# Scratch image by row, channel, column: fewer and longer runs into the patches of a depthwise convolution

## The chip, the cores and the metric

The kernel runs on one core of one Trainium2 chip. All data are float32. The metric is the time of one execution on the device in microseconds. The profile is of one execution, and its times count from its first instruction.

## The reference, cut to what matters

A batch of 16 images of 256 channels and 64 x 64 pixels goes through two layers. Layer 0 is a group norm, an RMS norm over channels, linear attention with four heads, an output projection, an RMS norm, and a residual. Layer 1 is a group norm and a mixture of four experts, of which a router picks two for each image; each expert is a depthwise 3 x 3 convolution, an exact GELU and a pointwise product over channels.

```python
def _expert(x, dw_k, dw_b, pw_k, pw_b):
    h = lax.conv_general_dilated(x, dw_k, window_strides=(1, 1), padding='SAME', feature_group_count=x.shape[1], ...)
    h = h + dw_b[None, :, None, None]
    h = jax.nn.gelu(h, approximate=False)
    h = jnp.einsum('bchw,oc->bohw', h, pw_k) + pw_b[None, :, None, None]
    return h
...
x = x + _L0_conv_ref(_gn(x), ...)
x = x + _L1_conv_ref(_gn(x), ...)
```

## The kernel before, in words

The work of an image is cut into phases, and up to several images are under way at once. Phase "in" takes the statistics of the first group norm, with loads `load_a` (tile xa, L945). Phase "q" normalises (`load_b`, tile xb, L948), projects and builds the attention's context. Phase "out" applies it and adds to the image, which stays in `ring` (loaded in L824). Phase "route" computes the router. Phases "c", "v" and "x" are layer 1, and its output is stored in L1483.

The 256 channels of the depthwise convolution are split. VectorE computes channels 128 to 255 with eight multiply-adds for each tile of 16 rows (`tap1`, L1436). TensorE computes channels 0 to 127 in phase "c", half an image (32 rows) at a time, h = 0 and 1:

- `pad0` writes the normalised rows of a half into `pd0`, with a border: 128 channels in the partitions, and in each 18 rows (`WR`) of 132 elements (`SW`). These 132 are two padded strips of 66, for the upper and the lower 16 rows of the half.
- `lay` (L1350) stores `pd0` in a scratch image in HBM, `lays[h]`.
- `spread` (L1359) reads the scratch image back into a patch buffer `xr`, so that the 3 x 3 window lies in the partitions: partition 18 dx + u holds row u shifted by dx columns, 54 partitions in all, for a group of channels; r = 0 and 1 put two groups of channels at partitions 0 and 64. Partition 54 keeps ones, for the bias.
- `conv0` (L1394) multiplies a channel's patch with the channel's banded tap matrix `taps`. One product gives 16 output rows for both chosen experts.
- `gelu0` (L1406), `put` (L1411) and `take` (L1422) apply GELU, store the result in a second scratch, `hids[h]`, and read it back with channels in the partitions as tile hp, which the pointwise products (L1465) use.

Before, `CB` is 16: a patch holds 16 channels at r = 0 and 16 at r = 1, so a half has `NU` = 4 patches. There are `NXR` = 2 patch buffers. A patch is read with six transfers, for each r and each dx, with 18 rows of 16 runs each; a run is 130 elements, 520 bytes.

All these transfers are issued by SyncE (SP) in one queue. The order of all instructions on all queues is written out: `rows` lists every step with a phase, an image and a key, `place` gives it a due time from the table `PLAN` (base values by key, and exceptions for single images), and the steps are issued in the order of these times. A unit of `PLAN` is a 64th of an image's period. The schedule is manual, so an engine never runs a step ahead of one that stands before it in its queue.

Of the kernel before, what the change touches and what calls it, by code (L numbers as in the profile page):

```python
# [10 lines left out]
FP = mybir.dt.float32  # L11
# [5 lines left out]
P = 128  # L17
# [11 lines left out]
QR = H // NQ  # L29
# [13 lines left out]
WR = QR + 2  # L43
WK = 3 * WR
KT = WK + 1
# [3 lines left out]
CB = 16  # L49
NU = P // (2 * CB)  # L50
NXR = 2
# [9 lines left out]
    "load_x1": 2.47, "mean": 6.06, "means": 12.14, "dev": 15.13, "devs": 17.94, "scale": 19.64,  # L61
    "bias": 22.84, "in_lead": 26.32, "norm0": -8.37, "norm1": -3.84, "turn_x0": 0.8, "x_sq0": 1.94,
    "x_sq1": 2.47, "turn_x1": 1.77, "x_sq2": 2.71, "x_sq3": 3.45, "token": 4.3, "x_keep0": 5.16,
    "x_keep1": 5.18, "x_keep2": 5.25, "x_keep3": 5.28, "project0": 3.33, "evacuate0": 5.95,
    "project1": 4.22, "evacuate1": 6.41, "project2": 4.36, "evacuate2": 6.69, "project3": 4.83,
    "evacuate3": 6.79, "context": 9.85, "q_sum": 8.95, "q_norm": 10.71, "q_turn": 14.88,
    "q_keep": 16.51, "mix_a": 10.1, "mix_turn": 10.19, "mix_v": 10.58, "mix_vv": 11.37,
    "mix_b": 11.59, "mix_out": 13.76, "mix_c": 14.28, "mix_lead": 16.01, "attend0": -1.55,
    "out_sq0": -0.08, "out_sq1": 0.23, "out_scale0": 0.69, "out_norm0": 2.07, "attend1": -0.02,
    "out_sq2": 1.36, "out_sq3": 1.4, "out_scale1": 2.39, "out_norm1": 3.75, "out_turn0": 5.8,  # L70
    "out_add0": 7.08, "sq_sums0": 8.58, "out_turn1": 6.3, "out_add1": 7.4, "sq_sums1": 9.3,
    "sums1": 10.09, "means1": 10.12, "scale1": 11.26, "router": 11.97, "route": 12.07,
    "choose": 13.45, "pick_taps": 21.11, "route_lead": 21.97, "weigh": 23.15, "pick_bias": 26.54,
    "pad1": -9.33, "start0": -0.79, "tap01": 1.45, "tap02": 1.68, "tap03": 2.04, "tap04": 2.27,
    "tap05": 2.38, "tap06": 5.02, "tap07": 5.53, "tap08": 6.45, "gelu10": 13.51, "start1": 2.19,
    "tap11": 3.82, "tap12": 8.44, "tap13": 8.46, "tap14": 9.11, "tap15": 9.48, "tap16": 12.72,
    "tap17": 13.76, "tap18": 14.53, "gelu11": 15.1, "pw00": 16.39, "pw01": 16.8, "pw02": 17.78,
    "pw03": 17.67, "pw10": 16.24, "pw11": 16.38, "pw12": 20.17, "pw13": 20.98, "residual00": 20.37,
    "residual01": 20.58, "store0": 32.42, "residual10": 22.66, "residual11": 22.95, "store1": 24.52,
    "in_first": 0.94, "in_more": 1.71, "q_first": 3.44, "out_first": 48.37, "out_more": 9.94,  # L80
    "q_less": 0.19, "load_a0": -17.65, "load_a1": -7.44, "load_b0": -16.6, "load_b1": -6.03,
    "stats0": -12.91, "stats1": -1.7, "load_weights": 29.84, "scale_weights": 28.54,
    "end_pw00": 102.59, "end_pw01": -70.76, "end_pw02": 22.48, "end_pw03": 218.26,
    "end_residual00": 0.34, "end_residual01": 51.45, "end_pw10": 154.95, "end_pw11": -20.19,
    "end_pw12": -67.04, "end_pw13": -35.14, "end_residual10": -34.02, "end_residual11": 60.24,
    "x_0": 0.93, "x_1": 0.16, "x_2": -0.1, "x_e1": 3.92, "x_e2": 4.69, "route_0": -3.24,
    "route_1": -0.18, "route_2": 0.26, "route_e1": -0.52, "route_e2": -0.36, "out_0": -5.57,
    "out_1": -0.5, "out_2": -0.02, "out_e1": -2.04, "out_e2": -0.91, "q_0": -6.4, "q_1": -1.79,
    "q_2": 0.02, "q_e1": -1.76, "q_e2": -0.97, "in_0": -31.7, "in_1": 8.38, "in_2": 3.12,
    "in_e1": -1.71, "in_e2": 0.13, "pw04": -118.21, "pw14": -3.07, "x_last": 16.29, "v_last": 15.03,  # L90
    "v_e1": 2.91, "tap18@e2.3": 12.85, "start0@e1.3": -3.52, "token@2.7": 3.88, "x_sq2@2.2": 3.74,
    "gelu11@e1.2": 14.77, "tap03@0.1": 1.16, "tap01@2.0": 1.08, "project0@0.0": 0.61,
    "out_norm1@2.7": 4.05, "out_sq1@e2.0": 0.67, "out_scale1@1.2": 2.97, "evacuate0@1.2": 5.59,
    "context@1.7": 8.56, "out_scale1@0.0": 4.31, "q_norm@0.0": 12.2, "out_turn0@1.4": 6.57,
    "mix_turn@0.7": 10.41, "token@2.1": 5.01, "out_sq3@1.6": 2.23, "project0@2.7": 4.76,
    "context@0.5": 10.29, "context@0.7": 8.85, "attend1@e1.3": -1.81, "out_norm1@1.1": 2.82,
    "context@2.1": 9.04, "q_norm@0.6": 10.76, "out_turn0@e1.5": 6.51, "out_norm0@1.1": 2.17,
    "gelu11@e2.3": 14.74, "evacuate2@1.7": 6.56, "out_norm1@0.6": 3.44, "evacuate2@2.2": 7.77,
    "project0@2.3": 2.36, "token@2.2": 3.83, "norm0@0.0": -11.77, "token@0.0": 2.08,
    "q_sum@0.0": 11.89, "x_sq2@2.6": 1.49, "norm1@0.0": -4.6, "out_norm1@e1.1": 3.47,  # L100
    "x_sq2@1.2": 3.52, "tap04@e2.2": 2.34, "x_keep0@0.5": 5.79, "out_turn0@1.2": 4.48,
    "evacuate3@1.7": 7.41, "q_sum@e2.4": 9.13, "x_sq2@2.5": 4.05, "turn_x0@0.0": -3.21,
    "out_scale0@1.2": 2.66, "tap13@2.0": 7.09, "x_keep3@1.2": 4.83, "mix_vv@2.7": 12.07,
    "out_turn0@1.3": 3.88, "q_sum@e2.6": 9.1, "x_sq2@0.0": 1.95, "scale1@0.0": 10.63,
    "token@0.1": 2.9, "q_sum@1.5": 10.12, "q_sum@1.1": 8.65, "tap12@e1.1": 4.38,
    "x_keep1@0.1": 7.82, "evacuate2@1.6": 5.85, "q_sum@1.3": 8.96, "out_turn0@2.6": 5.62,
    "out_turn0@1.1": 2.84, "route@0.0": 11.68, "x_sq2@1.4": 2.92, "q_turn@0.2": 14.91,
    "bias@0.7": 22.58, "token@1.4": 4.28, "pick_taps@e1.0": 15.29, "out_add0@2.5": 5.94,
    "means@0.7": -2.13, "dev@e2.7": 2.44, "evacuate3@1.2": 8.83, "x_sq3@1.4": 3.69,
    "x_keep1@0.7": 6.7, "mix_turn@1.7": 10.31, "x_sq2@2.7": 3.86, "x_sq3@2.5": 3.02,  # L110
    "mix_v@0.7": 10.76, "token@1.1": 4.28, "tap17@e2.3": 12.01, "out_turn0@e1.1": 6.18,
    "token@0.2": 5.57, "token@2.6": 5.19, "q_sum@1.2": 9.27, "out_norm0@1.2": 3.9,
    "x_keep0@0.7": 5.29, "mix_b@e1.7": 12.97, "choose@1.0": 15.45, "project0@e1.7": 3.62,
    "out_norm1@1.2": 4.35, "tap07@e1.2": 9.83, "tap11@e1.2": 5.06, "means@1.7": 3.63,
    "token@1.3": 3.21, "out_scale0@1.0": 2.27, "q_sum@e1.6": 9.24, "tap12@e2.0": 7.96,
    "out_scale1@e1.1": 1.65, "out_scale0@1.3": 0.78, "route@e1.0": 12.38, "x_sq2@1.5": 2.61,
    "pick_taps@2.0": 15.11, "out_turn0@1.0": 5.78, "scale@0.7": 19.8, "tap06@e1.0": 4.95,
    "out_turn1@e2.2": 7.26, "token@0.7": 4.82, "q_sum@e2.7": 9.92, "stats0@e2.5": -8.11,
    "tap13@e1.1": 5.09, "out_turn0@1.5": 6.39, "token@e1.5": 3.87, "token@1.6": 4.36,
    "q_turn@e2.1": 14.75, "out_norm1@e2.5": 2.7, "turn_x0@2.4": -0.38, "out_scale0@1.4": -1.04,  # L120
    "out_add1@0.5": 5.86, "out_add1@1.0": 8.63, "weigh@0.0": 25.58, "x_sq2@1.0": 2.93,
    "token@1.5": 3.15, "pick_bias@2.0": 25.19, "out_turn0@0.3": 6.25, "turn_x0@2.2": -2.86,
    "mix_b@0.7": 11.76, "out_scale1@e2.6": 2.43, "gelu11@e1.0": 17.17, "token@e2.7": 3.47,
    "out_sq3@0.6": 1.42, "context@1.2": 15.45, "q_sum@e2.0": 8.11, "tap01@e1.3": 0.02,
    "choose@e1.0": 13.66, "tap12@e2.2": 8.32, "x_keep0@0.1": 4.83, "x_sq2@1.6": 2.27,
    "load_a1@1.6": -8.35, "q_sum@0.1": 13.46, "q_sum@2.5": 10.2, "q_norm@0.2": 14.38,
    "tap13@e2.3": 7.78, "weigh@2.0": 20.53, "x_sq2@1.1": 2.49, "q_sum@e2.3": 9.79,
    "x_keep0@1.2": 9.93, "stats1@1.0": 2.95, "tap03@1.1": 1.88, "q_sum@1.0": 8.1,
    "q_turn@0.6": 13.24, "project1@2.2": 5.21, "token@1.2": 3.7, "context@1.4": 11.85,
    "mean@1.7": 0.59, "tap03@e1.2": -0.05, "x_sq3@2.7": 3.41, "x_keep2@0.4": 7.31, "token@2.4": 3.5,  # L130
    "q_turn@e2.3": 15.38, "mix_b@1.7": 12.57, "tap15@e1.2": 9.1, "out_sq3@e2.5": 1.53,
    "load_a1@1.4": -8.23, "x_sq3@1.6": 3.7, "pick_bias@1.0": 32.6, "q_sum@1.7": 8.15,
    "tap03@e1.3": 1.72, "out_norm1@0.7": 4.24, "choose@2.0": 13.4, "q_norm@0.3": 12.98,
    "out_turn0@0.1": 6.17, "x_keep1@0.5": 6.37, "out_turn0@e1.7": 7.03, "out_norm1@0.5": 3.66,
    "router@2.0": 11.71, "means1@e1.0": 10.8, "mean@0.7": -5.23, "project0@e2.7": 3.52,
    "x_keep0@1.7": 6.08, "context@1.3": 10.11, "router@0.0": 11.34, "tap17@e1.3": 15.47,
# [2110 lines left out]
```

## Time and profile before

| | |
|---|---|
| median of the runs | 2900.73 us (2875.53, 2900.73, 2912.88) |
| profiled execution: time, span | 2905.06 us, 2903.3 us |
| granted TensorE clock, mean | 0.929 |
| PE, DVE, ACT, POOL busy | 85%, 78%, 71%, 31% of the span |
| transfers of SP's queue (q1) | 498336 packets, 573.80 MB, 75.2% of 16 engines |
| HBM read, written | 400.94 MB, 175.24 MB |
| PE idle until a patch lands (xr<-lay) | 182.6 us in 64 waits |
| issue of one spread transfer on SP | 265 ns shortest, 742 median, 3787 longest |

The span reaches from the first to the last instruction. "A <- B" after a wait names who ended it; "DMA xr<-lay" is a transfer from lay to xr, and "SPq" is the time in which SP's queue issues or waits. A DMA share is the mean over 16 DMA engines, so it can hide that some of them are fuller than others. The chain that ended last is followed back from the last instruction; its shares say what the end of the program waited for.

### The profile page before, as it was taken

How to read it: one execution, taken by the hardware profiler on the slowest of the kernel's cores; microseconds unless marked ns; L12 is line 12 of the kernel's file. 1: busy time of each engine (PE TensorE's matmuls, PEld its weight loads, DVE VectorE, ACT ScalarE, POOL GpSimd, SP SyncE). 2: the span in 40 equal slices, each digit the busy share in tenths (PEclk: the TensorE clock that was granted, in tenths of full speed). 3: DMA queues.
4: the chain of work that ended last, by engine and by line, in shares of the span. 5: the costliest groups of instructions: out<-in, count | busy, mean ns of one | idle time of the engine just before them, and what ended most of it. 6: DMA issues, size and time to landing. Idle time of an engine off the chain costs nothing.

```text
span 2903.3 us, 49820 instructions
## 1 busy us (share of the span) xinstructions
PE 2478.1 (85%) x17204; PEld 1660.5 (57%) x17204; DVE 2255.1 (78%) x3489; ACT 2067.3 (71%) x4852; POOL 886.9 (31%) x1206
## 2 busy tenths in 40 slices
PE   6888888899788898888898888899889888896876
PEld 5775555566465666556566565566656556553432
DVE  7556787887778887888887778798887877677785
ACT  3697777787777887777687777788778778775432
POOL 4343243332223232232333223333223333232110
PEclk9998999999999999999999899999999999998888
DMA  4857887787877887887778887778788767777775
GB/s 136 128 160 185 210 209 192 206 222 206 215 190 211 218 222 211 221 212 198 212 206 227 208 209 203 204 222 222 214 228 215 196 186 190 180 180 193 196 190 153
DMA packets 531925, 579.57 MB, mean 200 GB/s; under 512 B 63184, under 2 KB 424144, under 8 KB 523472
## 3 DMA queue, kind: packets, MB, share of 16 engines
q1 hardware_dynamic: 498336, 573.80, 75.2%
q10 hardware_dynamic: 33328, 2.49, 1.5%
q8 instruction: 139, 2.28, 0.3%
q14 instruction: 122, 1.00, 0.1%
HBM read 400.94 MB, written 175.24 MB: 198 GB/s over the span
## 4 chain that ended last, share of the span: by engine, by line
DMA 32%; PE 30%; DVE 12%; ACT 9%; SPq 9%; issue 4%; POOL 3%; ACTq 0%; DVEq 0%; POOLq 0%
DMA xr<-lay 15%; PE pw L1465 10%; DMA hid<-hx 8%; SPq L1359 7%; DVE acc L1436 5%; DMA hp<-hid 5%; PE pq L1036 5%; PE dw L1394 4%; PE po L1130 4%; PE pc L1054 3%; PE px L1005 2%; DMA lay<-pd 1%; ACT junk L1138 1%; DMA xa<-in_x 1%; ACT hx L1406 1%
## 5 line engine op out<-in xcount | busy, mean ns | idle before, releaser
L1436 DVE SCALAR_TENSOR_TENSOR acc<-pd,ds,acc 128x1024 f32<-128x1024 f32 x1024 | 1325.8, 1299 | 79.3 <-ACT acc L1429 63.7
L1465 PE MATMUL pw<-acc,ps 128*128 128x512 f32 x1024 | 512.0, 635 | 31.2 <-ACT acc L1444 28.1
L929 POOL TENSOR_SCALAR s<-ss 128x2 f32<-128x2 f32 x256 | 117.6, 459 | 1366.3 <-ACT junk L1138 1363.2
L1465 PE MATMUL pw<-hp,ps 128*128 128x512 f32 x1024 | 495.4, 617 | 32.4 <-DMA hp<-hid 31.3
L1036 PE MATMUL pq<-wqkv_n,xg 128*128 128x256 f32 x2048 | 494.5, 386 | 13.1 <-DVE ring L1167 5.3
L1036 PEld LDWEIGHTS pq<-wqkv_n,xg 128*128 128x128 f32 x2048 | 383.0, 192 | 91.2 <-issue 20.0
L1138 ACT ACTIVATE junk<-po 128x256 f32<-128x256 f32 x512 | 198.2, 387 | 302.6 <-PE po L1130 283.6
L1394 PE MATMUL dw<-xr,taps 55*32 55x128 f32 x8192 | 209.8, 317 | 213.6 <-DMA xr<-lay 182.6
L1465 PEld LDWEIGHTS pw<-acc,ps 128*128 128x128 f32 x1024 | 195.1, 201 | 229.8 <-issue 154.1
L1465 PEld LDWEIGHTS pw<-hp,ps 128*128 128x128 f32 x1024 | 193.7, 198 | 229.7 <-issue 218.6
L1394 PEld LDWEIGHTS dw<-xr,taps 55*32 55x32 f32 x8192 | 153.4, 121 | 296.2 <-issue 194.9
L1130 PE MATMUL po<-mw,qt 128*128 128x256 f32 x1024 | 289.3, 410 | 12.1 <-ACT ob L1151 2.3
L1480 DVE SCALAR_TENSOR_TENSOR ring<-pw,bs,ring 128x512 f32<-128x512 f32 x248 | 181.8, 745 | 130.2 <-PE pw L1465 123.3
L1153 DVE TENSOR_TENSOR ob<-po,s 128x512 f32<-128x512 f32 x208 | 141.6, 682 | 159.5 <-POOL s L930 156.0
L1406 ACT ACTIVATE hx<-dw 128x512 f32<-128x512 f32 x256 | 149.8, 597 | 159.3 <-PE dw L1394 100.6
L1012 ACT ACTIVATE jx<-px 128x256 f32<-128x256 f32 x512 | 197.7, 386 | 85.4 <-PE px L1005 75.9
L1167 DVE SCALAR_TENSOR_TENSOR ring<-tr,gout,ring 128x512 f32<-128x512 f32 x256 | 186.3, 744 | 89.9 <-PE tr L1158 82.5
L1054 PE MATMUL pc<-xt,e 128*128 128x257 f32 x1024 | 253.1, 390 | 1.9 <-ACT xt L1023 1.4
L930 POOL TENSOR_TENSOR s<-s,mhalf 128x2 f32<-128x2 f32 x256 | 243.8, 952 | 21.3
L1130 PEld LDWEIGHTS po<-mw,qt 128*128 128x128 f32 x1024 | 195.5, 204 | 80.5 <-issue 38.4
L1044 ACT ACTIVATE e<-pq,r 128x256 f32<-128x256 f32 x512 | 210.5, 477 | 30.5 <-PE pq L1036 20.3
L1054 PEld LDWEIGHTS pc<-xt,e 128*128 128x128 f32 x1024 | 193.4, 196 | 34.4 <-issue 6.7
(145 smaller groups left out, 3562.3 us busy)
## 6 DMA issues: line engine op xcount, KB each, us to landing
xr<-lay SPq DMA_DIRECT2D x768, 146.2 KB
hid<-hx SPq DMA_DIRECT2D x256, 256.0 KB
hp<-hid SPq DMA_DIRECT2D x128, 512.0 KB
out<-ring SPq DMA_DIRECT2D x128, 512.0 KB
xa<-in_x SPq DMA_DIRECT2D x240, 256.0 KB
xb<-in_x SPq DMA_DIRECT2D x240, 256.0 KB
ring<-in_x SPq DMA_DIRECT2D x120, 512.0 KB
lay<-pd SPq DMA_DIRECT2D x32, 1188.0 KB
```

The lines of the kernel that those rows point to most:

```text
L930: nc.gpsimd.tensor_tensor(out_t, out_t, mhalf[:, :n], ALU.pow)
L1012: nc.scalar.activation(junk[:, :C], live["px", b, g, c // 2][:, c % 2], AF.Square, accum_out=ss[:, c : c + 1])
L1036: nc.tensor.matmul(pq, xg[:, k, c * P : (c + 1) * P], wqkv[:, k, : 2 * HID], start=(k == 0), stop=(k == KH - 1),)
L1044: nc.scalar.activation(live["e", b, g][:, c], live["pq", b, g, c // 2][:, c % 2], AF.Exp, scale=live["r", b, g][:, c : c + 1],)
L1054: nc.tensor.matmul(live["pc", b], live["e", b, g][:, c, HID:], xt[g % 2][:, c], start=(g == 0 and c == 0), stop=(g == NG - 1 and c == CG - 1),
L1130: nc.tensor.matmul(po[:, c], qt[:, n * P : (n + 1) * P], live["mw", b], start=True, stop=True)
L1138: nc.scalar.activation(junk[:, :C], live["po", b, g, hf][:, c], AF.Square, accum_out=ss[:, c : c + 1])
L1167: nc.vector.scalar_tensor_tensor(xin, live.pop(("tr", b, g, k)), gout[:, k : k + 1], xin, ALU.mult, ALU.add, accum_out=live["sm", b][:, 0, ...
L1359: nc.sync.dma_start(out=xr[(h * NU + v) % NXR][k0 : k0 + WR], in_=src[c0 : c0 + CB, :, dx : dx + SW - 2].rearrange("c u x -> u c x"),)
L1394: nc.tensor.matmul(pair[r][g * 2 * QR : (g + 1) * 2 * QR, s * HC : (s + 1) * HC], taps[ks, CB * v + i].rearrange("p i x -> p (i x)"), stri ...
L1436: nc.vector.scalar_tensor_tensor(acc, pd1[j % 2][:, t // 3 : t // 3 + QR, t % 3 : t % 3 + W], live["ds", b][:, i, t : t + 1], acc, ALU.mul ...
L1465: nc.tensor.matmul(po, w, rhs, start=begin, stop=end)
```

## The change

The scratch image is laid out by row, channel and column in place of channel, row and column. `lay` writes each channel's 18 rows to 18 places. In the new layout, eight channels of one row lie one after the other, 8 x 132 elements, so a row of a patch, shifted by dx, is one run of 1054 elements, 4216 bytes. A patch holds eight channels at each r, a half has eight patches, and there are four buffers. `spread` reads a patch with two transfers, one for each r, whose source steps over dx, then u, then the run, and whose destination is 54 partitions. `conv0` computes half of a pair of PSUM banks for each patch, and `put` still stores 16 channels at a time. The table `PLAN` has new values for nearly every key, and keys for the added patches; the lines shown are those of phase "c".

```diff
-CB = 16
+CB = 8
 NU = P // (2 * CB)
-NXR = 2
+NXR = 4
...
-    "lay": -4.49, "take00": 14.65, "take01": 13.96, "take10": 15.38, "take11": 16.26,
-    "c_lead": 0.53, "pad00": -8.92, "pad01": -7.63, "spread0": 2.48, "spread1": -1.79,
-    "spread2": 6.12, "spread3": 7.74, "conv0": 2.5, "gelu000": 4.29, "put00": 6.25, "gelu001": 4.71,
-    "put01": 6.61, "conv1": 5.01, "gelu010": 7.37, "put10": 8.3, "gelu011": 8.18, "put11": 9.1,
-    "conv2": 8.29, "gelu020": 10.86, "put20": 13.38, "gelu021": 10.21, "put21": 11.72,
-    "conv3": 12.34, "gelu030": 12.97, "put30": 14.03, "gelu031": 13.31, "put31": 14.24, "c_0": 0.71,
...
+    "pick11": 11.29, "lay": -3.67, "take00": 14.67, "take01": 12.36, "take10": 15.56,
+    "take11": 15.71, "c_lead": 0.55, "pad00": -9.35, "pad01": -7.2, "spread0": 1.78,
+    "spread1": -1.99, "spread2": -0.01, "spread3": 3.78, "spread4": 5.62, "spread5": 6.59,
+    "spread6": 7.67, "spread7": 7.97, "conv0": 2.42, "conv1": 2.77, "gelu000": 4.44, "put00": 5.71,
+    "gelu001": 5.41, "put01": 7.94, "conv2": 4.71, "conv3": 4.75, "gelu010": 6.6, "put10": 8.6,
+    "gelu011": 6.97, "put11": 10.06, "conv4": 8.45, "conv5": 8.51, "gelu020": 10.87, "put20": 12.36,
+    "gelu021": 10.39, "put21": 12.22, "conv6": 11.92, "conv7": 11.92, "gelu030": 12.14,
...
-    xr = [const.tile([P, CB, SW - 2], FP, name=f"xr_{i}") for i in range(NXR)]
+    xr = [const.tile([P, CB, SW], FP, name=f"xr_{i}") for i in range(NXR)]
...
-    lays = [hbm.tile([P, WR * SW], FP, tag=f"lay{h}", name=f"lay_{h}", bufs=1) for h in range(2)]
+    lays = [hbm.tile([WR, P, SW], FP, tag=f"lay{h}", name=f"lay_{h}", bufs=1) for h in range(2)]
...
     def lay(b, h):
-        nc.sync.dma_start(out=lays[h], in_=pd0.rearrange("p u a w -> p (u a w)"))
-
-    def spread(b, h, v):
-
-        src = lays[h].rearrange("p (u x) -> p u x", u=WR)
+        nc.sync.dma_start(
+            out=lays[h].rearrange("u p x -> p u x"), in_=pd0.rearrange("p u a w -> p u (a w)")
+        )
+
+    def spread(b, h, t):
+
+        n = CB * SW - 2
+        tile_t = xr[(h * NU + t) % NXR].rearrange("p c x -> p (c x)")
         for r in range(2):
-            c0 = r * P // 2 + CB * v
-            for dx in range(3):
-                k0 = r * P // 2 + dx * WR
-                nc.sync.dma_start(
-                    out=xr[(h * NU + v) % NXR][k0 : k0 + WR],
-                    in_=src[c0 : c0 + CB, :, dx : dx + SW - 2].rearrange("c u x -> u c x"),
-                )
+            c0 = r * P // 2 + CB * t
+            run = lays[h][:, c0 : c0 + CB].rearrange("u c x -> u (c x)")[:, :n]
+            nc.sync.dma_start(
+                out=tile_t[r * P // 2 : r * P // 2 + WK, :n],
+                in_=bass.AP(run.tensor, run.offset, [[1, 3], *run.ap]),
+            )
...
-    def conv0(b, h, v):
-
-        pair = [bank("dw", b, h, v, r) for r in range(2)]
-        live["dw", b, h, v] = pair
-        x = xr[(h * NU + v) % NXR]
-        for s in range(4):
-            for g in range(4):
-                i = 4 * s + g
-                for r in range(2):
...
+    def conv0(b, h, t):
+
+        v, n = divmod(t, 2)
+        if n == 0:
+            live["dw", b, h, v] = [bank("dw", b, h, v, r) for r in range(2)]
+        pair, x = live["dw", b, h, v], xr[(h * NU + t) % NXR]
+        for i in range(CB):
+            s, g = divmod(n * CB + i, 4)
+            for r in range(2):
...
     def put(b, h, v, r):
 
-        c0 = r * P // 2 + CB * v
+        c0 = r * P // 2 + 2 * CB * v
         nc.sync.dma_start(
-            out=hids[h][c0 : c0 + CB].rearrange("(s g) (k x) -> (g k) s x", g=4, x=HC),
+            out=hids[h][c0 : c0 + 2 * CB].rearrange("(s g) (k x) -> (g k) s x", g=4, x=HC),
...
-            for v in range(NU):
-                at("c", b, h, f"conv{v}", conv0, b, h, v)
+            for t in range(NU):
+                at("c", b, h, f"conv{t}", conv0, b, h, t)
+            for v in range(NU // 2):
```

## The prediction, made before the changed kernel was run

> **What bounds the kernel now.** I read the page from the top: shares, DMA totals, then the chain that ended last.
>
> ```profile
> span 2903.3 us, 49820 instructions
> ...
> PE 2478.1 (85%) x17204; PEld 1660.5 (57%) x17204; DVE 2255.1 (78%) x3489; ACT 2067.3 (71%) x4852; POOL 886.9 (31%) x1206
> ...
> DMA packets 531925, 579.57 MB, mean 200 GB/s; under 512 B 63184, under 2 KB 424144, under 8 KB 523472
> ...
> q1 hardware_dynamic: 498336, 573.80, 75.2%
> ...
> DMA 32%; PE 30%; DVE 12%; ACT 9%; SPq 9%; issue 4%; POOL 3%; ACTq 0%; DVEq 0%; POOLq 0%
> DMA xr<-lay 15%; PE pw L1465 10%; DMA hid<-hx 8%; SPq L1359 7%; DVE acc L1436 5%; DMA hp<-hid 5%; PE pq L1036 5%; PE dw L1394 4%; PE po L1130 4%; PE pc L1054 3%; PE px L1005 2%; DMA lay<-pd 1%; ACT junk L1138 1%; DMA xa<-in_x 1%; ACT hx L1406 1%
> ```
>
> No engine is full, but transfers hold 32% of the chain, and the largest is the one that changes: the spread, 15% in flight (xr<-lay) and 7% while SP issues it (L1359). So the spread holds 22% of 2903 us, 639 us, or 20 us in each of the 32 half images. Next, who waits for it: the group (busy time, mean ns, idle time before), then the waits of PE and of SP (total us, times, longest).
>
> ```profile
> L1394 PE MATMUL dw<-xr,taps 55*32 55x128 f32 x8192 | 209.8, 317 | 213.6 <-DMA xr<-lay 182.6
> ```
>
> ```profile
> PE dw L1394 <- DMA xr<-lay: 182.6, 64, 5.4
> ```
>
> ```profile
> SPq L1359 <- PE dw L1394: 117.3, 33, 8.6
> ```
>
> PE is idle 182.6 us for patches, 5.7 us a half: the largest DMA wait of PE, and the most that a perfect spread could save there. SP in turn waits 117.3 us for a conv to free a patch. Third, the DMA issues.
>
> ```profile
> xr<-lay SPq DMA_DIRECT2D x768, 146.2 KB
> hid<-hx SPq DMA_DIRECT2D x256, 256.0 KB
> ...
> lay<-pd SPq DMA_DIRECT2D x32, 1188.0 KB
> ```
>
> **How many engines a transfer uses.** This decides the case. Each transfer ends with a 4-byte packet on each engine that it ran on, and these can be counted. Under 512 B the page has 63184 packets. The data account for 32768 (the table, 64 B each), 2 x 512 (taps) and 2 x 512 (their biases), 512 (two norm weights) and 640 (router, biases): 35968. The rest is 27216. The issues are 768 spreads and 1269 others (all of 32, 64 or 128 rows on the outside), and 16 x 1269 + 9 x 768 = 27216 exactly. So a spread of 18 rows runs on nine engines, and all the others on sixteen: the largest divisor of the outer count up to 16.
>
> They are the same nine each time. In stretches where the spread moves almost alone, with several transfers queued, the windows say (last three columns: PE clock, DMA share, GB/s):
>
> ```profile
> 290.80:295.00 4.20, 3.71 (x18) 2.65 (x17) 4.13 (x6) 2.79 (x7) 1.88 (x3) 1.00 0.66 126
> 302.20:306.10 3.90, 3.90 (x15) 2.08 (x13) 3.81 (x6) 3.58 (x11) 0.10 (x2) 1.00 0.70 129
> 466.70:470.30 3.60, 3.60 (x15) 2.28 (x14) 3.56 (x8) 3.56 (x8) 1.72 (x3) 1.00 0.64 128
> ```
>
> Transfers that took turns over sixteen engines would fill them; here the share stays near 9/16 (packets overlap a little) and the rate near 125 GB/s.
>
> **The change, part by part.**
>
> *The spread's packets.* Removed: 768 transfers, 221184 packets of 520 B (115 MB). Added: 2 x 8 x 32 = 512 transfers of 54 packets of 4216 B (116.6 MB). Bytes stay. A 4096-byte packet takes 159 ns at the median of the trace's packet records and 195 ns in the mean, thus 164 to 201 ns for 4216 B. In sum over engines that is 27648 x 0.164 to 0.201 = 4500 to 5600 us against 221184 x 47.5 ns (mean record of a 520 B packet) = 10500 us: a saving of about half, if it were spread as now.
>
> *The spread's engines.* The new destination counts 54 rows, the new source counts [3][18][1054]: three shifts outermost. No transfer of before has outer counts that differ. The bounds are nine engines (54 cut as 18 is) and three (the source cut as its outer count says). I take three, because equal pieces must be the same bytes on both sides, and 3 is the only common divisor of both counts above 1. Then every patch's 108 packets lie on the same three engines, 36 each: 36 x 164 = 5.9 us per patch of eight channels, 47 us per half. Now a half is 24 transfers of 288 x 520 B, 3.6 MB, at 125 GB/s: 28.8 us. Three engines move 3 x 4096 B / 159 ns = 77 GB/s. The spread of a half grows by 47.2 - 28.8 = **18.4 us**, although its packets are better.
>
> [...]
>
> *Load of these three engines.* Per image each engine carries its sixteenth of all other traffic. By the records that is (34930 - 10500) / 16 / 16 = 95 us, where 34930 = 75.2% x 16 x 2903; with shortest typical packets (2048 B 84 ns, 4096 B 159, 512 B 27, 16384 B 611, 9504 B 362) it is 75 us. The spread adds 32 x 18 x 164 to 201 ns = 94 to 116 us. The three are needed 169 to 211 us per image; lay below adds 2 to 7. An image lasts 173 us now (first lay of image 0 at 199.6 us, of image 13 at 2451.5). Even filled without a gap, they allow no gain, and they become the fullest unit of the kernel.
>
> *Lay.* 32 transfers change from 128 packets of 9504 B to 2304 of 528 B. Nearest rows: 512 B out of SBUF 27 ns, 520 B 44 ns (median). Per engine 144 x 27 to 44 = 3.9 to 6.3 us against 8 x 362 ns = 2.9 us: 1.0 to 3.4 us a half, and the first patch waits for lay. I take 1.0, the 512 B row, since it goes the same way (SBUF to the scratch image).
>
> *SP.* 768 issues at a mean of 0.89 us (682 us, longest 3.8 us while packets pile up) become 512 with fewer packets. At the 0.41 us of a lay that is 210 us: up to 470 us of SP time freed. Queued behind are the loads xa and xb (L945, L948), the puts and the stores. I cost it at nothing: the spread's issue holds 7% of the chain because its packets pile up on their engines, and they pile up more on three. If the issue alone was the limit, it is worth up to 203 us (7%); that belongs to the first rival.
>
> *Costed at nothing:* eight convs of 16 matmuls instead of four of 32 (the same 8192 of 317 ns; PE's wait for patches covers the extra semaphores, some 0.05 us for each of 128 more); the start's memsets (four of half size; they ran at 16.8 us, long before the first patch at 208 us); the larger scratch rows. Four buffers of eight channels hold what two of sixteen held, so no more is fetched ahead. The order: in the middle images SP has spread1, spread2, spread0, then conv0 due, so three patches, 18 us, must land before the first conv, against two, 14 us, now. Bounds for the order alone: minus 183 us (all of PE's patch wait) to plus 128 us (these 4 us x 32); the value taken is 0, as the sum above already bills the transfers.
>
> **Sum.** 639 us of the chain against 28.8 x 32 = 922 us of spreading means that 0.7 of it is exposed. With the same share, 18.4 x 0.7 = 12.9 us, plus 0.7 us of lay: 13.6 x 32 = 435 us. 2903 + 435 = 3338, taken as **3340 us**: 200 us an image, at which the three engines would be busy for 171 to 218, so they would be close to full. The profiled execution took 2905 us, 1.8 around its span; the median of the runs is 2901, so no correction is made. The upper end: all of 18.4 + 3.4 us is exposed, 698 us, 3601. The lower: the engines' need of 174 us (169 + about 5 for lay) met at 95% use, 183 us an image, 16 x 10 = 160 us, 3065.
>
> **Rivals.**
> *Nine engines (faster), 10%.* If the cut follows the 54 rows, the spread of a half is 47.2 / 3 = 16 us. PE's 182.6 us go, lay costs up to 109: 2903 - 183 + 32 to 109 = 2752 to 2830; part of SP's 203 us may come on top. I put it at **2790 us**. For it: 18 rows do run on nine. Against it: an outer count of 3 cannot be shared by nine. It decides if the spread's rate stays over some 120 GB/s.
> *Three engines, but hidden (no difference), 6%.* PE has other work between the convs, and waits only 5.7 us a half. If the new order starts the patches so early that the three engines never rest, 169 to 174 us an image fit into 173: **2920 us**. Against it: the spreads' order gives them the same stretch of a half (from lay to the last conv 15.6 plan units, 16.8 before).
>
> **Numbers.** My forecast (slower) has 84%, the rivals 10 (faster) and 6 (same). The range 3040 to 3620 takes in both bounds of the forecast with some 20 us beyond each, and leaves out both rivals, 16%. Runs of before lie from 2876 to 2913, so 2% is about what can be told from no change.
>
> **What would show it.** Right: under 512 B there are 35968 + 20304 + 3 x 512 = 57808 packets (nine engines: 60880). Packets in all fall by some 129000, the DMA share falls although the kernel is slower, windows of spread alone show some 77 GB/s and a share near 0.2, and PE's wait for xr grows from 183 us to over 500. The waits for xb, xa and hp grow too, since they need all engines. The step on engines is wrong if the spread runs above 120 GB/s; the step on exposure is wrong if it runs at 77 and PE's wait stays under 300. A wait for lay over 10 us a half would show the 528 B rows as the larger cost.

## The result, and the profile after

| | before | after |
|---|---|---|
| median of the runs | 2906.81 us (2875.53 to 2921.09) | 3544.74 us (3542.09 to 3547.56) |
| after / before | | 1.224, 95% interval 1.214 to 1.234 |
| span of the profiled execution | 2903.3 us | 3541.7 us |
| granted TensorE clock, mean | 0.929 | 0.856 |

The medians here are over the four runs that each kernel had side by side. The change makes the kernel 22% slower. The forecast had the direction and the mechanism; its time, 3340 us, is 205 us short.

The page of the kernel after, from shares to the chain that ended last (the lines are those shown of before, and the row of the granted clock in 40 slices, in tenths):

```profile
span 3541.7 us, 49516 instructions
...
PE 2655.4 (75%) x17204; PEld 1758.2 (50%) x17204; DVE 2243.6 (63%) x3489; ACT 2067.3 (58%) x4848; POOL 907.1 (26%) x1208
...
PEclk9988878888888989888989888888888898886877
...
DMA packets 402644, 581.08 MB, mean 164 GB/s; under 512 B 57808, under 2 KB 271312, under 8 KB 398288
...
q1 hardware_dynamic: 369056, 575.32, 54.4%
...
DMA 49%; PE 22%; DVE 11%; ACT 6%; SPq 4%; issue 4%; POOL 4%; ACTq 0%; DVEq 0%; POOLq 0%
DMA xr<-lay 32%; PE pw L1499 8%; DMA hid<-hx 7%; DVE acc L1470 5%; DMA out<-ring 4%; PE pq L1068 4%; SPq L1393 3%; PE dw L1428 2%; PE pc L1086 2%; DMA lay<-pd 2%; PE px L1037 2%; PE po L1162 2%; DMA xb<-in_x 1%; DVE ring L1514 1%; DVE st L986 1%
```

57808 packets under 512 B is the count worked out for three engines, to the packet. Packets in all fall by 129281, and the share of q1 falls from 75.2% to 54.4%: the transfers have become far better by the page's totals, and the kernel is slower. The chain says why. The spread in flight (xr<-lay) rises from 15% to 32%, its issue on SP (L1393, before L1359) falls from 7% to 3%. Together they held 22% of 2903 us, 639 us, and now 35% of 3542 us, 1240 us: 601 us more, nearly all of the 638 us that the span grew. The two parts move apart: the flight grows by 698 us (435 to 1133), and the issue shrinks by 97 us (203 to 106).

The group of the conv that reads the patches (busy time, mean ns of one, idle time before and what ended it):

```profile
L1428 PE MATMUL dw<-xr,taps 55*32 55x128 f32 x8192 | 288.4, 351 | 690.0 <-DMA xr<-lay 617.3
```

The same 8192 matmuls now follow 690.0 us of idle time, 617.3 of it ended by a patch landing; before it was 213.6 and 182.6. Each takes 351 ns instead of 317; the clock comes to that below.

Three stretches in which the spread moves alone (busy us of PE, PEld, DVE, ACT, POOL with their instructions, PE clock, DMA share, GB/s):

```profile
1134.30:1143.80 9.50, 5.08 (x78) 3.70 (x77) 3.53 (x5) 5.61 (x11) 0.00 (x0) 0.74 0.20 81
1554.40:1563.90 9.50, 6.81 (x89) 5.03 (x88) 6.21 (x9) 5.61 (x11) 0.00 (x0) 0.91 0.20 82
2186.10:2195.50 9.40, 6.71 (x88) 5.07 (x87) 6.11 (x9) 5.61 (x11) 0.00 (x0) 0.90 0.19 78
```

About 80 GB/s at a share of 0.20: three of sixteen engines are 0.19. Before, such stretches read 126 to 129 GB/s at 0.64 to 0.70. This is the plainest sign in the profile, and no total shows it.

Who else waits for transfers (total us, times, longest), of any engine and then of SP's own queue:

```profile
PE dw L1428 <- DMA xr<-lay: 617.3, 215, 12.8
...
ACT hx L1440 <- DMA hid<-hx: 293.9, 75, 10.7
...
DVE st L986 <- DMA xa<-in_x: 98.8, 19, 16.3
...
PE pw L1499 <- DMA hp<-hid: 9.1, 7, 3.7
```

```profile
SPq L856 <- DMA out<-ring: 353.1, 54, 10.7
SPq L1393 <- PE dw L1428: 207.5, 70, 6.7
...
SPq L1393 <- DMA lay<-pd: 81.5, 24, 7.0
```

Before, the two of these that grew most read:

```profile
ACT hx L1406 <- DMA hid<-hx: 53.6, 37, 5.8
```

```profile
SPq L824 <- DMA out<-ring: 77.4, 22, 8.1
```

Transfers that share the queue come later too: the store of hid, whose landing frees the buffer that ACT writes next, and the load of xa (before 28.7 us). The wait for hp shrank, from 31.3 us to 9.1. Before it loads the next image into `ring` (L856, before the change L824), SP now stands 353.1 us until the store of the output has landed. The spread on the same engines may be a part of that; it is not all, since the same wait is 233.2 us in e2 below, which uses nine engines. Lay, in its new rows, holds up SP's spreads for 81.5 us in all (before 45.3), 2.5 us a half: it is not what made the kernel slow.

### The profile page after: what moved, and what is told of

The parts are those of the page before. It is cut to its first block, busy times and chain, and to the rows that moved or that the text cites. A ratio compares the mean times of both kernels' runs of the same rounds, so it can differ in the third digit from the quotient of the medians.

```text
span 3541.7 us, 49516 instructions
## 1 busy us (share of the span) xinstructions
PE 2655.4 (75%) x17204; PEld 1758.2 (50%) x17204; DVE 2243.6 (63%) x3489; ACT 2067.3 (58%) x4848; POOL 907.1 (26%) x1208
## 2 busy tenths in 40 slices
DMA packets 402644, 581.08 MB, mean 164 GB/s; under 512 B 57808, under 2 KB 271312, under 8 KB 398288
## 3 DMA queue, kind: packets, MB, share of 16 engines
q1 hardware_dynamic: 369056, 575.32, 54.4%
## 4 chain that ended last, share of the span: by engine, by line
DMA 49%; PE 22%; DVE 11%; ACT 6%; SPq 4%; issue 4%; POOL 4%; ACTq 0%; DVEq 0%; POOLq 0%
DMA xr<-lay 32%; PE pw L1499 8%; DMA hid<-hx 7%; DVE acc L1470 5%; DMA out<-ring 4%; PE pq L1068 4%; SPq L1393 3%; PE dw L1428 2%; PE pc L1086 2%; DMA lay<-pd 2%; PE px L1037 2%; PE po L1162 2%; DMA xb<-in_x 1%; DVE ring L1514 1%; DVE st L986 1%
## 5 line engine op out<-in xcount | busy, mean ns | idle before, releaser
L1428 PE MATMUL dw<-xr,taps 55*32 55x128 f32 x8192 | 288.4, 351 | 690.0 <-DMA xr<-lay 617.3
L1428 PEld LDWEIGHTS dw<-xr,taps 55*32 55x32 f32 x8192 | 169.6, 132 | 826.3 <-issue 374.0
L961 POOL TENSOR_SCALAR s<-ss 128x2 f32<-128x2 f32 x256 | 132.4, 517 | 1518.3 <-ACT junk L1170 1515.6
L1499 PE MATMUL pw<-hp,ps 128*128 128x512 f32 x1024 | 503.5, 628 | 17.9 <-DMA hp<-hid 9.1
L1499 PE MATMUL pw<-acc,ps 128*128 128x512 f32 x1024 | 502.1, 625 | 19.6 <-ACT acc L1478 13.8
L1068 PEld LDWEIGHTS pq<-wqkv_n,xg 128*128 128x128 f32 x2048 | 392.9, 197 | 103.4 <-issue 20.8
L1514 DVE SCALAR_TENSOR_TENSOR ring<-pw,bs,ring 128x512 f32<-128x512 f32 x248 | 179.5, 745 | 375.1 <-PE pw L1499 372.1
L1086 PE MATMUL pc<-xt,e 128*128 128x257 f32 x1024 | 279.8, 421 | 3.5 <-DVE xt L1053 1.5
L962 POOL TENSOR_TENSOR s<-s,mhalf 128x2 f32<-128x2 f32 x256 | 261.6, 1022 | 21.3
L1086 PEld LDWEIGHTS pc<-xt,e 128*128 128x128 f32 x1024 | 212.6, 216 | 40.3 <-issue 3.8
L986 DVE BATCH_NORM_STATS2 st<-xa 128x6 f32<-128x512 f32 x240 | 163.0, 681 | 99.0 <-DMA xa<-in_x 98.8
```

The source lines that it names most:

```text
L962: nc.gpsimd.tensor_tensor(out_t, out_t, mhalf[:, :n], ALU.pow)
L986: nc.vector.bn_stats(st[:, k, g], live.pop(("xa", b, g, k)) if b else x1(b, g)[:, k])
L1068: nc.tensor.matmul(pq, xg[:, k, c * P : (c + 1) * P], wqkv[:, k, : 2 * HID], start=(k == 0), stop=(k == KH - 1),)
L1086: nc.tensor.matmul(live["pc", b], live["e", b, g][:, c, HID:], xt[g % 2][:, c], start=(g == 0 and c == 0), stop=(g == NG - 1 and c == CG - 1),
L1428: nc.tensor.matmul(pair[r][g * 2 * QR : (g + 1) * 2 * QR, s * HC : (s + 1) * HC], taps[ks, CB * t + i].rearrange("p i x -> p (i x)"), stri ...
L1499: nc.tensor.matmul(po, w, rhs, start=begin, stop=end)
```

## The experiments

Each run is compared with the kernel before, run on the same chip beside it; ratios are this kernel over before, with a 95% interval. "After" is 3545 us throughout. Before measured 2888 to 2890 us beside these runs and 2907 beside after, so times of different runs are compared only to some 20 us.

### Three engines or nine, all else as in after

**e2_nine_one** swaps two dimensions: a patch's partition is 3u + dx instead of 18dx + u, so the source counts [18][3][1054] and the outer count is 18. The bands, which say which partition meets which tap, follow. Transfers, bytes, packets of 4216 B and order are those of after.

```diff
-                at0 = (dx * WR + dy) * QR
+                at0 = (3 * dy + dx) * QR
...
-                    te[:, :, at0 : at0 + (QR - 1) * (QR + 1) + 1 : QR + 1],
+                    te[:, :, at0 : at0 + (QR - 1) * (3 * QR + 1) + 1 : 3 * QR + 1],
...
-                in_=bass.AP(run.tensor, run.offset, [[1, 3], *run.ap]),
+                in_=bass.AP(run.tensor, run.offset, [run.ap[0], [1, 3], *run.ap[1:]]),
```

> As the changed kernel, still one transfer of 54 rows for each r, but partition 3u + dx holds row u shifted by dx (the tap table is laid out to match), so the source counts [18][3] instead of [3][18]. Theory of three engines, set by the common divisor of the outer counts: 18 and 54 give nine, 60880 packets under 512 B, and a time as with six transfers or up to 30 us less, since SP issues 512 transfers instead of 1536: 2740 to 2830 us. Rival, that a destination of 54 rows is itself the cause: 57808 packets, 3540 us.

Measured: **2650.67 us**, 0.917 (0.914 to 0.920). Its page, its conv group, and three stretches of spread alone:

```profile
span 2648.4 us, 49516 instructions
...
PE 2394.2 (90%) x17204; PEld 1602.0 (60%) x17204; DVE 2239.9 (85%) x3489; ACT 2060.4 (78%) x4848; POOL 923.0 (35%) x1208
...
DMA packets 405716, 581.10 MB, mean 219 GB/s; under 512 B 60880, under 2 KB 274384, under 8 KB 401360
...
PE 33%; DMA 18%; DVE 18%; ACT 11%; issue 5%; POOL 4%; SPq 2%; ACTq 0%; POOLq 0%; DVEq 0%
PE pw L1499 16%; DVE acc L1470 9%; DMA xr<-lay 8%; DMA hid<-hx 5%; PE pq L1068 4%; PE po L1162 3%; PE pc L1086 3%; PE dw L1428 2%; PE tr L1190 2%; PE px L1037 2%; DVE ring L1514 2%; DMA out<-ring 1%; ACT junk L1170 1%; DVE ob L1185 1%; DVE st L986 1%
```

```profile
L1428 PE MATMUL dw<-xr,taps 55*32 55x128 f32 x8192 | 180.1, 280 | 50.6 <-DMA xr<-lay 39.7
```

```profile
1952.00:1955.00 3.00, 3.00 (x8) 1.61 (x7) 0.85 (x3) 3.00 (x6) 2.28 (x3) 0.57 0.59 198
244.00:247.50 3.50, 3.19 (x17) 2.51 (x15) 0.00 (x0) 3.26 (x7) 0.00 (x0) 1.00 0.57 190
2473.50:2476.50 3.00, 3.00 (x14) 1.89 (x13) 3.00 (x4) 1.98 (x6) 0.45 (x1) 1.00 0.56 171
```

60880 packets under 512 B: 57808 + 512 x 6, so each of the 512 transfers now runs on nine engines. PE's wait for patches falls from 617.3 us to 39.7, the spread alone moves 171 to 198 GB/s instead of 80, and the kernel is 894 us faster than after by this alone, and faster than before. A packet of 4216 B takes 164 ns at the median in both kernels, so it is the number of engines, and not a slower packet, that sets them apart. This settles the cause: nothing else of the change has to be undone.

**e1_nine_six** gets nine engines another way: after's layout, but one transfer for each shift, of 18 rows.

```diff
-            nc.sync.dma_start(
-                out=tile_t[r * P // 2 : r * P // 2 + WK, :n],
-                in_=bass.AP(run.tensor, run.offset, [[1, 3], *run.ap]),
-            )
+            for dx in range(3):
+                k0 = r * P // 2 + dx * WR
+                nc.sync.dma_start(
+                    out=tile_t[k0 : k0 + WR, :n],
+                    in_=bass.AP(run.tensor, run.offset + dx, [*run.ap]),
+                )
```

> The changed kernel (scratch layout, runs of 4216 B, patches of eight channels, order), with the patch read by one transfer for each shift: 18 rows on both sides, six transfers a patch. Theory of three engines: 18 rows go to nine engines, a patch costs each 2 x 3 x 2 packets of 164 ns = 2.0 us instead of 5.9, a half 15.7 us instead of 47.2, so the kernel is faster than before, 2750 to 2830 us, and PE's wait for xr is under 100 us. Rival, the order and the smaller patches: they stay, so it stays over 3300 us. Rival, the 528 B rows of lay: stays over 3300 us too, with waits for lay over 10 us a half.

Measured: 2726.28 us, 0.944 (0.941 to 0.946); PE waits 28.3 us for patches. It is 76 us slower than e2, with three times the transfers, and still beats both kernels given.

**e6_three_old_order** asks whether three engines are slow under the order of before as well. Before, with patches of 16 channels in its own order, but the scratch image and the source [3][18] of after (packets of 8440 B).

```diff
-    xr = [const.tile([P, CB, SW - 2], FP, name=f"xr_{i}") for i in range(NXR)]
+    xr = [const.tile([P, CB, SW], FP, name=f"xr_{i}") for i in range(NXR)]
-    lays = [hbm.tile([P, WR * SW], FP, tag=f"lay{h}", name=f"lay_{h}", bufs=1) for h in range(2)]
+    lays = [hbm.tile([WR, P, SW], FP, tag=f"lay{h}", name=f"lay_{h}", bufs=1) for h in range(2)]
...
-            for dx in range(3):
-                k0 = r * P // 2 + dx * WR
-                nc.sync.dma_start(
-                    out=xr[(h * NU + v) % NXR][k0 : k0 + WR],
-                    in_=src[c0 : c0 + CB, :, dx : dx + SW - 2].rearrange("c u x -> u c x"),
-                )
+            run = lays[h][:, c0 : c0 + CB].rearrange("u c x -> u (c x)")[:, :n]
+            nc.sync.dma_start(
+                out=tile_t[r * P // 2 : r * P // 2 + WK, :n],
+                in_=bass.AP(run.tensor, run.offset, [[1, 3], *run.ap]),
+            )
```

> The kernel before, with its order and its two buffers of 16 channels, but with the scratch by row, channel, column and one transfer of 54 rows for each r, source [3][18], runs of 8440 B. Theory of three engines: the same 47.2 us a half on three engines, so it is slow in the old order too, 3400 to 3600 us. Rival, the new order and the smaller patches: about 2900 us.

Measured: 3589.68 us, 1.242 (1.239 to 1.245). PE's wait for patches:

```profile
PE dw L1396 <- DMA xr<-lay: 743.7, 148, 13.5
```

So the loss needs neither the new order nor the smaller patches; with them it is 45 us smaller.

### How much of a longer spread is exposed

Three runs put loads between nine and three engines on the spread.

**e3_six** keeps e2's partitions, but reads six rows u at a time: source [6][3], 18 partitions, three transfers for each r, which run on six engines (a half takes 47.2 / 2 = 23.6 us).

```diff
-            nc.sync.dma_start(
-                out=tile_t[r * P // 2 : r * P // 2 + WK, :n],
-                in_=bass.AP(run.tensor, run.offset, [run.ap[0], [1, 3], *run.ap[1:]]),
-            )
+            for u0 in range(0, WR, 6):
+                k0 = r * P // 2 + 3 * u0
+                part = run[u0 : u0 + 6]
+                nc.sync.dma_start(
+                    out=tile_t[k0 : k0 + 18, :n],
+                    in_=bass.AP(part.tensor, part.offset, [part.ap[0], [1, 3], *part.ap[1:]]),
+                )
```

> As the kernel with partition 3u + dx, but each r is read by three transfers of six image rows, [6][3] against 18: six engines by the divisor. A half costs each engine 8 x 2 x 9 packets of 164 ns = 23.6 us, less than the 28.8 us of the kernel before. Theory of three engines: 2800 to 2900 us, near the nine-engine time, since the spread is no longer the fullest unit. [...]

Measured: 3109.05 us, 1.076 (1.073 to 1.078), some 200 us more than expected. Its packets under 512 B, 65488, are those of six engines, so that part held. The chain by line, and the issue of the spread on SP (shortest, median and longest ns, first to last us):

```profile
SPq L1396 12%; PE pw L1502 10%; DMA xr<-lay 9%; DVE acc L1473 8%; DMA hid<-hx 7%; PE pq L1068 3%; PE dw L1431 3%; PE pc L1086 2%; PE po L1162 2%; DMA hp<-hid 2%; DMA lay<-pd 2%; PE tr L1190 2%; PE px L1037 2%; DVE ring L1517 1%; DMA out<-ring 1%
```

```profile
L1396 SPq DMA_DIRECT2D xr<-lay x1536: 690/692/1732, 217.2 to 3066.1; - x192
```

The issue on SP leads the chain. No issue took less than 690 ns, and 1536 of them held SP for 1098 us. So the run doesn't measure six engines alone; it measures SP as well. In e1 the same number of transfers, also into 18 rows, but with an 18-row source, took:

```profile
L1395 SPq DMA_DIRECT2D xr<-lay x1536: 264/307/1513, 216.0 to 2672.5; - x192
```

**e8_half_read** has the load of six engines without their issues: after, with three engines, but the patches of the second group (r = 1) are not read, so the conv reads stale data for those channels. 256 transfers, 23.6 us a half.

```diff
-        for r in range(2):
+        for r in range(1):
```

> The changed kernel with three engines, but the patches of r = 1 are not read (that half of the channels is computed from what stands in the buffers): a half then costs the three engines 23.6 us, the same as six engines with the whole read, with 256 transfers to issue instead of 1536. If the load of the engines sets the time: straight between 15.7 us (2651) and 47.2 us (3545) it is 2875 us; flat up to some load and then wholly exposed it is 2790 us. If six engines were slow (3109 us) by their load and not by the issue of 1536 transfers of 0.7 us on SP, it is near 3100 us.

Measured: 2773.09 us, 0.961 (0.957 to 0.964). **e10_three_quarters** leaves out r = 1 for every second patch only: 384 transfers, 35.4 us a half.

```diff
-        for r in range(2):
+        for r in range(2 - t % 2):
```

> The changed kernel with three engines, but r = 1 is not read for the odd patches: 35.4 us a half on the three engines. If each further us of spread is wholly exposed, as between 23.6 us (2773) and 47.2 us (3545): 2773 + 11.8 x 32 x 1.02 = 3158 us. If the three engines hold the kernel back only once they are full: under 3000 us.

Measured: 3183.40 us, 1.103 (1.099 to 1.107). PE's waits for patches in e8 and in e10 (total us, times, longest):

```profile
PE dw L1428 <- DMA xr<-lay: 90.8, 65, 6.3
```

```profile
PE dw L1428 <- DMA xr<-lay: 349.0, 146, 11.3
```

| kernel | spread of a half, us | time, us | slope to the row above |
|---|---|---|---|
| e2_nine_one | 15.7 | 2651 | |
| e8_half_read | 23.6 | 2773 | 122 / (7.9 x 32) = 0.48 |
| e10_three_quarters | 35.4 | 3183 | 410 / (11.8 x 32) = 1.09 |
| after | 47.2 | 3545 | 362 / (11.8 x 32) = 0.96 |

The slopes are not pure: e8 and e10 also issue less. At 0.7 us an issue, and 0.38 us of time for each us of SP (e11 below), the 128 issues between e8, e10 and after are worth up to 34 us a row, and the 256 between e2 and e8 up to 68 us the other way. With them taken out the slopes are 0.75, 0.99 and 0.87.

Nor are the loads: the table counts 164 ns for every packet, the median. In the mean a 4216 B packet took 212 ns in e2, 183 in e8, 184 in e10 and 180 in after, so a half takes 20.3, 26.4, 39.8 and 51.7 us, and the slopes are 0.63, 0.96 and 0.95, or 0.97, 0.88 and 0.86 with the issues taken out. Every way a us more of spreading costs about one us (0.86 to 1.09) from e8's load on. Below it the slope is not pinned: 0.48 to 0.97.

The order of before says the same: e4 (below) and e6 share the layout and the order, with 28.8 and 47.2 us a half, and lie 667 us apart, although e6's issues held SP for 375 us less. That is 1.13 of 18.4 x 32 = 589 us.

### What an issue on SP costs

**e11_twice_the_issues** is e2 with each transfer cut into two of four channels. Bytes and engines stay; the issues double, and so do the spread's packets (of 2.1 KB).

```diff
+        hc = CB // 2
-        n = CB * SW - 2
+        n = hc * SW
...
+            for s in range(2):
+                c0 = r * P // 2 + CB * t + hc * s
+                m = n - 2 * s
+                run = lays[h][:, c0 : c0 + hc].rearrange("u c x -> u (c x)")[:, :m]
```

> The kernel of 2651 us (nine engines, 54 rows, new order), with each transfer cut into two of four channels: runs of 2112 B, 1024 issues instead of 512, the same bytes on the same engines. An issue of this form held SP for 0.69 to 0.77 us, so SP is held some 375 us longer. If that was the reason why six engines with 1536 issues took 3109 us and half the read on three 2773 us (336 us for 703 us of SP): 2651 + 180 = 2830 us. If the issues are hidden: 2650 to 2680 us.

Measured: 2795.47 us, 0.969 (0.965 to 0.973). The issues of e2 and of e11:

```profile
L1393 SPq DMA_DIRECT2D xr<-lay x512: 731/757/1084, 216.9 to 2599.4; - x171
```

```profile
L1396 SPq DMA_DIRECT2D xr<-lay x1024: 731/737/1487, 217.5 to 2741.2; - x171
```

The spread held SP for 395 us in e2 and for 776 us here: 145 us of time for 381 us of SP, 0.38 for one. PE's wait for patches hardly moves (39.7 to 53.4 us). What comes late is other work of SP; the wait that grew most is ACT's for the store of hid, in e2 and in e11:

```profile
ACT hx L1440 <- DMA hid<-hx: 69.1, 43, 4.8
```

```profile
ACT hx L1443 <- DMA hid<-hx: 149.7, 72, 7.0
```

The smaller packets may have a part in the 145; the run can't separate that. The expectation set the 336 us between e3 and e8 against 703 us of SP, which is what e3 holds more than e2. Against e8, which held SP for 212 us, it is 886 us: 0.38 for one as well.

### The parts of the change that had been billed low or at nothing

**e4_lay_only**: before, with lay in rows of 528 B (the scratch image by row, channel, column), and the spread reading its 520 B runs from there.

```diff
-        nc.sync.dma_start(out=lays[h], in_=pd0.rearrange("p u a w -> p (u a w)"))
+        nc.sync.dma_start(
+            out=lays[h].rearrange("u p x -> p u x"), in_=pd0.rearrange("p u a w -> p u (a w)")
+        )
...
-                    in_=src[c0 : c0 + CB, :, dx : dx + SW - 2].rearrange("c u x -> u c x"),
+                    in_=lays[h][:, c0 : c0 + CB, dx : dx + SW - 2],
```

> The kernel before, with the scratch by row, channel, column only: lay writes 2304 rows of 528 B, and the spread still reads runs of 520 B with six transfers of 18 rows in the old order. In the changed kernel a 528 B packet took 35 ns in the mean, so a lay costs each engine 144 x 35 ns = 5.0 us instead of 2.9. If that is exposed: 2.1 x 32 = 67 us, 2950 to 2970 us. Rival, it is hidden by other transfers: within 1% of before. Rival, the 528 B rows are the costly part of the change: over 3100 us.

Measured: 2922.96 us, 1.014 (1.009 to 1.018): 39 us more (0.0136 of some 2884; by the interval 26 to 52), between the 22 us billed in the sum and the 109 us of its upper end.

**e5_old_order_long**: e4, with long runs (8440 B) to 18 rows: 16 channels, the old order, three transfers for each r, nine engines.

```diff
-                    out=xr[(h * NU + v) % NXR][k0 : k0 + WR],
-                    in_=lays[h][:, c0 : c0 + CB, dx : dx + SW - 2],
+                    out=tile_t[k0 : k0 + WR, :n],
+                    in_=bass.AP(run.tensor, run.offset + dx, [*run.ap]),
```

> The kernel before with its order, its buffers of 16 channels and six transfers a patch, but long runs (8440 B) from the scratch by row, channel, column; nine engines. Theory: longer packets on the same nine engines bring the gain, and the order little: 2700 to 2780 us, as the kernel with six transfers in the new order (2726 us). Rival, the new order brings it: 2850 us or more.

Measured: 2786.94 us, 0.965 (0.961 to 0.969), 136 us less than e4 and 7 us above the expected range. The spread's issue:

```profile
L1363 SPq DMA_DIRECT2D xr<-lay x768: 264/292/1292, 209.8 to 2733.9; - x192
```

Median 292 ns, 234 us in all, where e4 needed 655 us and before 682. Stretches of spread alone (columns as above):

```profile
2048.60:2052.30 3.70, 3.24 (x70) 1.62 (x68) 1.78 (x2) 3.61 (x10) 2.74 (x4) 1.00 0.61 155
1120.70:1123.60 2.90, 2.90 (x11) 1.25 (x9) 2.85 (x7) 2.90 (x5) 2.30 (x3) 1.00 0.57 157
2216.40:2219.40 3.00, 3.00 (x22) 1.62 (x28) 1.85 (x3) 2.97 (x7) 0.93 (x2) 1.00 0.57 159
```

155 to 159 GB/s on nine engines (a share of 0.57 to 0.61), where 520 B runs gave 126 to 129 in the three stretches of the prediction and 124 to 139 over six. So long runs do make transfers of 18 rows faster, by about a fifth, and they free SP. On the chain the issue of the spread falls from 7% of 2917 us in e4 to no more than 2% here (all of SP's share), and the spread in flight goes from 13% to 16% of 2786 us. The run changes both at once, so their shares of the 136 us stay open.

**e7_old_order_nine_one**: e5's patches in one transfer for each r, cut to nine engines as in e2.

```diff
-            for dx in range(3):
-                k0 = r * P // 2 + dx * WR
-                nc.sync.dma_start(
-                    out=tile_t[k0 : k0 + WR, :n],
-                    in_=bass.AP(run.tensor, run.offset + dx, [*run.ap]),
-                )
+            nc.sync.dma_start(
+                out=tile_t[r * P // 2 : r * P // 2 + WK, :n],
+                in_=bass.AP(run.tensor, run.offset, [run.ap[0], [1, 3], *run.ap[1:]]),
+            )
```

> The kernel before with its order and its buffers of 16 channels, long runs, partition 3u + dx, and one transfer of 54 rows for each r on nine engines. Theory: as the new order on nine engines (2651 us), within 2%: 2620 to 2700 us. Rival, the new order and smaller patches carry a part of the gain: over 2720 us.

Measured: 2811.23 us, 0.972 (0.969 to 0.976): well above the expectation, and 160 us above e2. PE still waits 152.8 us for patches. **e9_small_old_order** parts the two things that lie between: e2 with eight-channel patches in four buffers, but due at the times that before's table gave to the sixteen-channel ones (both halves of one together). Against e2 only the table changes; these are the lines of its base values that show it.

```diff
-    "spread0": 1.78, "spread1": -1.99, "spread2": -0.01, "spread3": 3.78, ...
+    "spread0": 2.48, "spread1": 2.48, "spread2": -1.79, "spread3": -1.79, ...
...
-    "conv0": 2.42, "conv1": 2.77, "conv2": 4.71, "conv3": 4.75, ...
+    "conv0": 2.5, "conv1": 2.5, "conv2": 5.01, "conv3": 5.01, ...
```

> Patches of eight channels in four buffers, partition 3u + dx, one transfer of 54 rows for each r on nine engines (all as in the kernel of 2651 us), but the order of the kernel before: the old table, with both halves of an old patch due together, when the old one was. The same engines with 16-channel patches in the old order took 2811 us. If the smaller patches are what is worth 160 us: 2640 to 2700 us. If the new order is: 2780 to 2830 us.

Measured: 2703.02 us, 0.935 (0.931 to 0.939), with 60.8 us of waiting for patches. So of the 160 us the smaller patches bring 108 (2811 to 2703) and the new order 52 (2703 to 2651). The smaller patches are also smaller packets, 4216 B for 8440: e7's stretches of spread alone moved 161 to 168 GB/s, for example

```profile
220.60:224.80 4.20, 4.20 (x65) 3.45 (x50) 4.13 (x6) 2.66 (x10) 1.07 (x2) 0.50 0.58 161
```

where e2 moved 171 to 198. How much of the 108 us is that rate, and how much the earlier start of a conv that needs half as much, no run here separates.

## Why the prediction was right, and where it was short

**The engines.** Right, and shown. The count of packets is the one worked out; e2 changes which dimension comes first and nothing of size, and time falls from 3545 to 2651 us; e6 has three engines without the rest of the change and is as slow as after. Counting the short packets in the trace of before was enough to find it. Its stretch of spread alone from 302.20 to 306.10 us has one to 33 packets of 520 B (29 to 964), where nine to the 288 of a transfer are one to 32:

```profile
DMA packets 993, 0.50 MB, mean 129 GB/s; under 512 B 29, under 2 KB 993, under 8 KB 993
```

At each shape run here the count fits the largest number up to 16 that divides both outer counts: [3][18] against 54 rows took three engines (57808 packets under 512 B in after), [6][3] against 18 six (65488 in e3), [18][3] against 54 nine (60880 in e2), 18 against 18 nine (70096 in e1). The reason given, that equal pieces must be the same bytes on both sides, was the author's argument; no run shows it. The first rival, the cut along the 54 rows, was wrong for this change.

**Packets and rate.** Right. 164 ns is the median record of a 4216 B packet after as well (mean 179.5), and three engines moved 78 to 82 GB/s where 77 was given. What held before's nine engines near 125 GB/s was, at least in part, the 520 B packet: e5 moved 155 to 159 GB/s with transfers of 18 rows on nine engines as well.

**The exposure: the step that failed.** The sum took 18.4 us more a half and exposed 0.7 of it, because 0.7 of before's spreading was exposed on average. That is an average; the question was what the next us costs. The 0.7 was also not one thing: its 639 us of the chain hold 203 us of issue on SP, and the flight alone was 435 of 922 us, 0.47. From one lay to the next an image took 173.2 us before and takes 213.6 after: 20.2 us more a half, not 13.6. The chain gained 601 us of spread (698 in flight, less 97 of issue), against 18.4 x 32 = 589 us. The runs put a number on it: 0.86 to 1.09 from 23.6 us a half on in the new order, and 1.13 from before's 28.8 us on in the old one (e4 to e6). So next to nothing of the addition was hidden. The 0.7 should have been taken as a floor and the upper bound, "all of it exposed", as the value: 2903 + 589 + 22 = 3514 us, 31 us below the result.

**Lay.** Billed 22 us, measured 39 (e4). A small miss, of the size of what was left.

**SP.** Costed at nothing, which was right for this kernel, since the issue still held SP for 725 us (before 682), but only in part for the reason given. Transfers do pile up (mean 1.42 us, longest 7.6): by the packet records of after, the 239 issues with three or more spread transfers still to land took 1.85 us at the median, the 273 others 0.70. Still, half of the 725 us is there without that, as 512 issues at the median of 0.71 us. But the size of what could be freed, down to 210 us at 0.41 us each, was wrong. Even with nine engines e2's 512 issues took 395 us, 0.77 us each.

**The order and the smaller patches.** Costed at 0 within -183 to +128. They bring 45 us with three engines (e6 to after) and 160 us with nine (e7 to e2). That a patch half as large lets the conv start sooner, if the spread is not itself the bound, is likely, but not shown apart from the packets' rate.

**The rival with nine engines** was put at 2790 us, from 2752 to 2830. Where nine engines were really had, it was 2651 (e2) and 2726 (e1): below its range. PE's wait fell by 143 us (182.6 to 39.7), lay cost 39, and what is left is not told apart: the smaller patches and the order (108 and 52 us by e7, e9 and e2), SP's time, of which the rival had named 203 us as a possible bonus, and PE's clock.

**The clock.** Not in the prediction. The granted clock falls from 0.929 to 0.856 after, and rises to 0.971 in e2, with PE's busy time at 2478, 2655 and 2394 us for the same instructions. In the trace's clock records it is full or half; half of it adds up to 413 us before, 1022 us after and 157 us in e2. Half-clock spells come after more idleness than usual: in the 7 us before one, PE was idle 3.2 us on average in after, against 1.8 us at any time (its busy share is 75%), and 2.9 us in before, against 1.0. So the clock seems to follow the waits and to make them somewhat dearer, though no run shows what sets it; PE's share of the chain fell meanwhile, from 30% of 2903 us (871 us) to 22% of 3542 (779 us). How much of the 601 us it feeds, no run here separates.

**The signs named.** Count of packets, fall of all packets, lower DMA share, 77 GB/s at 0.2, PE's wait over 500 us (617.3): as said. Of the waits for xb, xa and hp, only xa's grew clearly; xb's stayed (18.3 to 19.5 us) and hp's fell. The wait of an engine that grew most beside the patch's, that for hid (53.6 to 293.9 us), had not been named.

## What to carry to other kernels

Before merging transfers, write down the outer counts of both sides and ask how many engines they leave: here [3][18] or [18][3] for the same 54 rows was 3545 or 2651 us. Count the short completion packets in the profile and look at a stretch where the transfer runs alone; the totals of packets and of share improved in the slow kernel. For a longer transfer on a path that already waits for it, bill the whole addition, and keep the average exposure for the lower end.

## What the runs showed of the hardware that was not expected

- **What an issue on SP costs depends on the form of the two sides.** Where source and destination have the same row counts, an issue took 292 to 307 ns at the median (e5, e1). Where they are [3][18] or [18][3] against 54, or [6][3] against 18, none took less than 671, 731 and 690 ns (after, e2, e3), even with 18 packets only. e5 and e3 both fill 18 rows with 18 packets, so the number of packets is not the reason; what is, stays open. Before's spreads have equal row counts, and their shortest issue, 265 ns, is as short; that their median was 742 goes with transfers piling up: by the packet records, the 383 issues of before with fewer than three spread transfers still to land took 377 ns at the median, the 385 others 1102. The median of e4 is much the same (768).
- **Nine engines are not worth the same for every transfer.** In stretches of spread alone they moved 124 to 139 GB/s with 520 B packets to 18 rows (before), 155 to 159 with 8440 B to 18 rows (e5), 161 to 168 with 8440 B to 54 rows (e7), and 171 to 198 with 4216 B to 54 rows (e2). At 164 ns a packet nine engines would move 231. What holds them below that is open. It is not the packet alone: 8440 B took 319 ns at the median on three engines (e6) and 478 on nine (e7), with 54 rows both times.
- **SP's time is worth something even where patches are in time**: 145 us of time for 381 us of issues in e11, while PE waited little longer for patches than in e2 (53.4 and 39.7 us).
